# A planned instruction order, with transfers that hold the queue by their size and later assumed landings

## The chip, the cores and the metric

The kernel runs on one core of a Trainium2 chip. The metric is device time in microseconds; three runs of the kernel before gave 2084.32, 2087.18 and 2086.25 us, median 2086.25. One further execution was recorded by the hardware profiler.

## The reference, cut to what matters

128 graphs of 128 nodes with 256 features go through two layers. In layer 0 three rounds of a gated graph network run on `h`, and in layer 1 an attention over edges:

```python
h = relu(layernorm(x))
for i in range(3):                                   # layer 0
    m    = einsum('bnd,de->bne', h, weight[i])
    aggr = einsum('bst,bsd->btd', adj != 0, m)
    h    = gru_cell(aggr, h, w_ih, w_hh, b_ih, b_hh)
x = x + h
h  = relu(layernorm(x))                              # layer 1
Wh = h @ W ; s = Wh.sum(-1)
e  = where(adj == 0, -inf, leaky_relu(s[:, :, None] + s[:, None, :], 0.2))
x  = x + einsum('bpq,bqo->bpo', softmax(e), Wh)
```

## The kernel before, in words

The graphs are taken in 32 groups of four (`G = 4`). A group's node rows are 128 x 1024 float32 (512 KB) in a tile `rows`, its edges 256 KB in `at`; later `x` is read a second time into `x1` for the residual sum, and `x1` is written out (512 KB). Every round of a group is one "turn" on TensorE: products of node features with weights (L887 and L901) in seven-product blocks, which build up in the PSUM banks `x_rz, x_n, y_rz, y_n, q_rz, q_n`; ScalarE copies a bank out (L933, L937, L939) before TensorE may write it again. Edge sums are the 128x128 bf16 products of L807; the attention's products are L840 and L1326. The list `turns` interleaves the rounds: a group's round 0, the previous group's round 1 and the round 2 of the group before that follow one another.

Layer norms (`normed`, L686 to L702) run on VectorE (bn_stats, L686, four to a group), GpSimd (L695, L696) and ScalarE (L702). In the attention of a group VectorE reduces the scores to their maximum (L1243), negates a bounded form of it into `low` (L1245), ScalarE takes exponentials (L1250), copies them in halves into `pe` (L1422), a transfer transposes them (L1423, `peT`), and ScalarE unpacks them (L1426). Feature halves are transposed in the same way through `pl` and `plT` (L743, L753, L747). All transfers, transposes included, are issued by SyncE (SP), in one queue.

Nothing of the order is left to a scheduler at run time. `Plan.op` records each operation with its engine, its duration in ns, the tiles it reads and writes and a due time. `Plan.search` then tries many list schedules with random changes of rank (fixed seed), in windows, and keeps the one with the least idle TensorE, plus a tenth of `risk` (how far a TensorE operation has less than `SLACK` = 1500 ns of reserve); near the end, the modelled end counts too. The instructions are emitted in that order, and each engine runs its own in order. So a number in the plan changes no instruction, only places in five queues.

The lines that the change touches are those that say when a transfer's result may be used. An operation on SP holds the queue for its `ns`. Its users start no earlier than its end plus a lag (3600 ns where none is given) plus 28 ns. Landings are kept apart by a constant:

```python
FLIP, HANDOFF, COLD, BEHIND = 56, 120, 7200, 1200            # L57, in Plan
def wait(self, i, u):                                        # L141
    a, b = self.nodes[i], self.nodes[u][0]
    return 0 if a[0] == b == "PE" else a[7] + self.SIGNAL[b]
if e == "SP":                                                # L323, in go
    late = max(s.landed + self.BEHIND - done - n[7], 0)
    s.landed = done + n[7] + late
```

The loads of a group's `rows` and `at` are L1112 (L502 for the first four groups, `TIMED`), the second reading of `x` is L1131, the transposes L753 and L1423, the weight loads L502 and L571.

Of the kernel before, what the change touches and what calls it, by code (L numbers as in the profile page):

```python
# [16 lines left out]
P = 128  # L17
# [14 lines left out]
FIRST, LAST, COMMIT, AHEAD, SLACK, RISK = 20000, 120000, 32000, 40000, 1500, 0.1  # L32
TIMED = 4
KB = 3
GATES = 18150
BIG = 3.0e38

# [9 lines left out]
class Plan:  # L47
# [7 lines left out]
    LAG = {"PE": 163, "ACT": 0, "DVE": 0, "POOL": 0, "SP": 3600}  # L55
    OVER = {"PE": 0, "ACT": 50, "DVE": 40, "POOL": 0, "SP": 0}
    TRUE = {"PE": 0, "ACT": 103, "DVE": 84, "POOL": 42, "SP": 0}  # L57
    FLIP, HANDOFF, COLD, BEHIND = 56, 120, 7200, 1200
    SIGNAL = {"PE": 53, "ACT": 36, "DVE": 36, "POOL": 78, "SP": 28}

    def __init__(self, tags):
# [30 lines left out]
        return deps  # L92

    def op(self, eng, ns, fn, reads=(), writes=(), room=(), due=None, mark=None,
           turn=None, two=False, lag=None, thin=False):

        i, deps = len(self.nodes), set()  # L100
        self.group_of.append(self.group)
        for item in room:
            b, lo, hi = item if isinstance(item, tuple) else (item, 0, 1 << 30)
            if self.tags[b.tag][1] == "ring":
                self.rooms.append((i, b, lo, hi))
            elif b.prev is not None:
                deps.update(self.over(b, lo, hi))
        for is_write, group in ((False, reads), (True, writes)):
            for item in group:
                b, lo, hi = item if isinstance(item, tuple) else (item, 0, 1 << 30)  # L110
                for j, w, l, h in b.accesses:
                    if (w or is_write) and l < hi and lo < h:
                        deps.add(j)
                if is_write and b.prev is not None:
                    deps.update(self.over(b, lo, hi))
        for is_write, group in ((False, reads), (True, writes)):
            for item in group:
                b, lo, hi = item if isinstance(item, tuple) else (item, 0, 1 << 30)
                b.accesses.append((i, is_write, lo, hi))
        deps.discard(i)  # L120
        bufs = {id(x[0] if isinstance(x, tuple) else x): (x[0] if isinstance(x, tuple) else x)
                for x in list(reads) + list(writes) + list(room)
                if self.tags[(x[0] if isinstance(x, tuple) else x).tag][1] in ("free", "turn")}
        free = [b for b in bufs.values() if self.tags[b.tag][1] in ("free", "turn")]
        for b in free:
            b.users.append(i)
            b.left += 1
        self.nodes.append([eng, ns, fn, deps, free, self.due if due is None else due,
                           two or eng == "POOL", self.LAG[eng] if lag is None else lag, thin])
        if due is not None:  # L130
            self.chain.append(i)
        if mark is not None:
            self.marks[mark] = i
        if turn is not None:
            self.turns.append((i, turn))
# [2 lines left out]

        return self.nodes[i][1] * (2 if self.nodes[i][0] == "PE" and t < self.COLD else 1)

    def wait(self, i, u):  # L141

        a, b = self.nodes[i], self.nodes[u][0]
        return 0 if a[0] == b == "PE" else a[7] + self.SIGNAL[b]

    def run(self):
        nodes, self.queue = self.nodes, {}
# [99 lines left out]
    def go(self, s, until):  # L247

        nodes, users, bound, order_of = self.nodes, self.users, self.bound, self.others
        rank, slots, at, clock, ready = s.rank, s.slots, s.at, s.clock, s.ready  # L250
        inf = float("inf")
        while len(s.order) < len(nodes) and clock["PE"] < until:
            best = None
            nxt = order_of[s.chain] if s.chain < len(order_of) else None
            for e, pool in ready.items():
# [3 lines left out]
                c = clock[e]  # L259
                for i in pool:  # L260
                    n = nodes[i]
                    if i in bound and i != nxt:
                        continue
                    t = max(c + (self.FLIP if s.thin and e == "PE" and not n[8] else 0), at[i])
                    if n[4]:
                        new = {}
                        for b in n[4]:
                            if id(b) not in s.slot:
                                new[b.tag] = new.get(b.tag, -1) + 1
                                t = max(t, sorted(slots[b.tag])[new[b.tag]])  # L270
                                if b.tag in self.queue and self.queue[b.tag][s.turn[b.tag]] is not b:
                                    t = inf
# [6 lines left out]
                asked, i = min(((r, i) for t, r, i in starts if t <= first), key=lambda x: (rank[x[1]], x[1]))  # L279
# [5 lines left out]
            t, _, e, i = best  # L285
# [3 lines left out]
            n = nodes[i]  # L289
            asked, cause, kind = s.other[i] if e == "PE" else at[i], s.due_to[i], "dep"  # L290
            done = t + self.ns(i, t)
            for b in n[4]:
                if id(b) not in s.slot:
                    if b.tag in self.queue:
                        s.turn[b.tag] += 1
                    k = min(range(len(slots[b.tag])), key=lambda k: slots[b.tag][k])
# [24 lines left out]
            s.end = max(s.end, done)  # L321
            late = 0
            if e == "SP":  # L323
                late = max(s.landed + self.BEHIND - done - n[7], 0)
                s.landed = done + n[7] + late
            for u in users[i]:
                s.missing[u] -= 1
# [41 lines left out]
def kernel(  # L369
# [21 lines left out]
    nc = tc.nc  # L391
# [58 lines left out]
    def ap(b):  # L450
        return phys[(b.tag,) + b.slot]
# [12 lines left out]
    op, buf = plan.op, plan.buf  # L464
# [32 lines left out]
        plan.group = SETS - 1  # L497
        return buf(tag)

    def load(dst, get, src, kb, behind=(), lag=3300):  # L500

        op("SP", kb * KB, lambda: nc.sync.dma_start(get(dst), src), behind, [dst], lag=lag)  # L502

    def plain(b):
        t = ap(b)
# [47 lines left out]
    def weights():  # L553
# [5 lines left out]
            return plain(b).rearrange("p (k e) -> p k e", k=KD)  # L559

        def load_msg(layer, behind=()):
            load(w_msg[layer], square, weight[layer].rearrange("(k p) e -> p k e", p=P), 256,
                 behind)


        plan.due = -2 * 10 ** 9
# [2 lines left out]
        for a in range(2):  # L569
            part = slice(3 * a, 3 * a + 3)  # L570
            op("SP", 384 * KB, lambda part=part: nc.sync.dma_start(  # L571
                nat(w_ih_nat)[:, part], w_ih.rearrange("(c p) e -> p c e", p=P)[:, part]),
               [], [(w_ih_nat, a, a + 1)], lag=3300 + 700 * a)
        plan.due = 10 ** 9
        load(w_hh_nat, nat, w_hh.rearrange("(c p) e -> p c e", p=P), 768, lag=5000)
        plan.due = -10 ** 8
        load_msg(1)
        plan.due = 10 ** 9
# [172 lines left out]
    def transpose(pl, plT, k, n):  # L751

        op("SP", 1283, lambda: nc.sync.dma_start_transpose(  # L753
            ap(plT)[:, k, 0:n].rearrange("p c (m q) -> p (c m) q", q=P),
            ap(pl)[:, k, 0:n].rearrange("p c m -> p (c m)")), [(pl, k, k + 1)], [(plT, k, k + 1)],
           lag=2200)

    def parts_of(rows):

# [342 lines left out]
    def group(g):  # L1102
        graphs = slice(g * G, (g + 1) * G)
        plan.phase = phase(g, 0)
        plan.due = (plan.phase - 1) * SLOT
        rows0, at, a, hT = buf("rows"), buf("at"), buf("a"), buf("hT")
        for t, src, kb in ((rows0, x[graphs].rearrange("b n d -> n b d"), 512),
                           (at, adj[graphs].rearrange("b n m -> n b m"), 256)):
            if g < TIMED:
                load(t, ap, src, kb, lag=4800 if t is at else 3300)  # L1110
            else:
                op("SP", 480, lambda t=t, src=src: nc.sync.dma_start(ap(t), src), [], [t])  # L1112
        op("DVE", 420, lambda: nc.vector.tensor_scalar(ap(a), ap(at), 0.0, None,
                                                       op0=OP.not_equal), [at], [a], two=True)
        plan.due = (phase(g, L - 1) + 2) * SLOT
        normed(rows0, rows0)
        for layer in range(L):
            plan.phase = phase(g, layer)
            if layer == 0:
                if g < EARLY:  # L1120
                    rows_to_T(rows0, hT)
                else:
                    turned_halves(rows0, True, hT)
                parts = parts_of(rows0) if g >= WHOLE else (rows0, buf("r1"))
            elif layer < L - 1:
                parts = turned_parts(hT)
            else:
                rows, x1, h1 = buf("rows"), buf("x1"), buf("h1")
                turned_halves(hT, False, rows)
                parts = parts_of(rows)  # L1130
                op("SP", 480, lambda: nc.sync.dma_start(  # L1131
                    ap(x1), x[graphs].rearrange("b n d -> n b d")), [], [x1])
            hs, aT, gs = buf("hs"), buf("aT"), buf("gs")
            node_sums(hT, hs, "POOL", 1272, 730)
            edge_sums(parts, a, aT)
            node_sums(aT, gs, "DVE", 690, 426)
            plan.cursor = plan.phase * SLOT
            if layer < L - 1:
                gru(layer, hT, hs, aT, gs)
        plan.due = min(phase(g, L - 1) + 3, len(turns) + 0.5) * SLOT  # L1140
        gru_rows(L - 1, hT, hs, aT, gs, rows, x1)
        if g < NG - 1:
            attention(g, lambda: edges_of(g, a), x1, h1, 0, G)
        else:
            scores = edges_of(g, a)
            for lo, hi in ((G // 2, G), (0, G // 2)):
                attention(g, lambda: scores, x1, h1, lo, hi)
# [271 lines left out]
    def turned_halves_of(halves, src, dst):  # L1419

        pe, peT = buf("pe"), buf("peT")
        op("ACT", 1045, lambda: nc.scalar.copy(ap(pe), halves()), [src], [pe])  # L1422
        op("SP", 1283, lambda: nc.sync.dma_start_transpose(  # L1423
            ap(peT).rearrange("p two g q -> p (two g) q"),
            ap(pe).rearrange("p two g m -> p (two g m)")), [pe], [peT], lag=2200)
        op("ACT", 1347, lambda: nc.scalar.copy(halves_of_blocks(dst), ap(peT)), [peT], [dst])  # L1426

    weights()
# [34 lines left out]
```

## Time and profile before

| what | us |
|---|---|
| median of three runs | 2086.25 |
| profiled execution, its time | 2087.59 |
| profiled execution, span from first to last instruction | 2085.5 |
| TensorE matmul busy | 2069.2 |
| VectorE / ScalarE / GpSimd busy | 1688.3 / 1619.1 / 910.0 |
| issue to landing, median: `rows` 512 KB | 5.1 |
| the same: second reading `x` 512 KB | 4.3 |
| the same: `at` 256 KB | 2.8 |
| the same: transposes plT / peT | 3.3 / 3.2 |

Busy time of TensorE includes modelled ends of pipelined matmuls, so a short gap can be partly covered by them; where it matters, gaps are read from start to start. In lists of waits the columns are: engine and line that waited, what released it, microseconds in total, times, longest. In a timeline or chain they are start, length, then the work; a bracket holds the idle time before it and its releaser. The stretch table gives, for each stretch, its length, then busy time and number of instructions of TensorE matmuls, TensorE weight loads, VectorE, ScalarE and GpSimd, the granted TensorE clock, the DMA share and GB/s.

### The profile page before, as it was taken

To read this page: it belongs to the slowest core of one execution; us is meant where nothing else is said; L and a number is where in the kernel's file an instruction comes from. 1 tells how busy PE (TensorE), PEld (TensorE's weight loads), DVE (VectorE), ACT (ScalarE), POOL (GpSimd) and SP (SyncE) were. 2 spreads that over 40 slices of the span, in tenths; PEclk is the share of its full clock that TensorE was granted. 3 is DMA by queue.
4 is the path that set the end of the run, shared out by engine and by line. 5 is a ranking of instruction groups with operands and counts; after the bars stand their busy time and mean duration, and the time that the engine had idled before them with its cause. 6 is when DMAs were issued, how large, how long until landed. Compare 5 with 4: busy or idle time off the path is not lost.

```text
span 2085.5 us, 31660 instructions
## 1 busy us (share of the span) xinstructions
PE 2069.2 (99%) x10926; PEld 1660.3 (80%) x10926; DVE 1688.3 (81%) x3912; ACT 1619.1 (78%) x3007; POOL 910.0 (44%) x885
## 2 busy tenths in 40 slices
PE   9999999999999999999999999999999999999998
PEld 7887887778877778877788877788777888788875
DVE  6777887888878888887888887888888877788677
ACT  6677887788877788877888777878777886878775
POOL 4644544435434435444354434454443544445330
PEclk9999999999999999999999999999999999999999
DMA  5322233332333323233222333232333223323321
GB/s 147 66 64 43 56 69 72 73 69 43 69 74 71 76 47 71 61 79 73 65 49 66 82 66 76 49 64 66 76 76 61 46 67 77 61 44 67 64 66 36
DMA packets 369376, 138.12 MB, mean 66 GB/s; under 512 B 300608, under 2 KB 368960, under 8 KB 369216
## 3 DMA queue, kind: packets, MB, share of 16 engines
q1 hardware_dynamic: 369216, 136.10, 29.6%
q8 instruction: 86, 1.41, 0.3%
q14 instruction: 74, 0.61, 0.1%
HBM read 45.36 MB, written 16.78 MB: 30 GB/s over the span
## 4 chain that ended last, share of the span: by engine, by line
PE 94%; DMA 2%; ACT 1%; DVE 1%; POOL 1%; SPq 0%; issue 0%; ACTq 0%; DVEq 0%; POOLq 0%
PE y_rz L887 15%; PE q_rz L887 10%; PE x_rz L887 10%; PE y_n L887 7%; PE misc L807 6%; PE y_n L901 6%; PE y_rz L901 6%; PE q_n L887 5%; PE x_n L887 5%; PE misc L1326 4%; PE x_n L901 4%; PE q_n L901 4%; PE x_rz L901 4%; PE q_rz L901 4%; PE misc L840 3%; DMA rows<-in_x_dram 2%
## 5 line engine op out<-in xcount | busy, mean ns | idle before, releaser
L856 POOL TENSOR_TENSOR hs<-hT 128x512 f32<-128x512 f32 x96 | 123.0, 1282 | 466.4 <-PE y_n L901 244.9
L764 POOL TENSOR_TENSOR r<-rows 128x512 f32<-128x512 f32 x126 | 137.7, 1111 | 173.0 <-ACT rows L702 91.0
L887 PE MATMUL y_rz<-hs,s_hh 128*128 128x256 f32 x768 | 197.7, 380 | 3.6 <-ACT t_rz L933 3.6
L887 PE MATMUL y_rz<-gs,s_x 128*128 128x256 f32 x768 | 197.2, 379 | 0.0
L943 DVE TENSOR_TENSOR t_rz<-t_rz,q_rz 128x512 f32<-128x512 f32 x192 | 131.4, 684 | 77.2 <-ACT t_rz L933 55.6
L933 ACT COPY t_rz<-y_rz 128x512 f32<-128x512 f32 x192 | 112.0, 583 | 99.9 <-PE y_rz L901 60.7
L887 PEld LDWEIGHTS y_rz<-hs,s_hh 128*128 128x128 f32 x768 | 145.3, 190 | 25.4 <-POOL rs L695 2.8
L860 POOL TENSOR_TENSOR hs<-hT,hs 128x256 f32<-128x256 f32 x96 | 77.6, 809 | 198.2 <-PE q_n L901 160.1
L887 PEld LDWEIGHTS y_rz<-gs,s_x 128*128 128x128 f32 x768 | 145.9, 190 | 19.6
L767 POOL TENSOR_TENSOR p<-r 128x512 bf16<-128x512 f32 x126 | 155.1, 1248 | 2.7
L943 DVE TENSOR_TENSOR t_n<-t_n,q_n 128x512 f32<-128x512 f32 x192 | 131.1, 683 | 29.5 <-PE q_n L901 17.1
L1081 POOL TENSOR_TENSOR x<-x,u 128x512 f32<-128x512 f32 x60 | 78.8, 1315 | 139.6 <-ACT u L1061 139.6
L887 PE MATMUL x_rz<-aT,s_x 128*128 128x256 f32 x512 | 131.5, 379 | 0.0
L887 PE MATMUL x_rz<-hT,s_hh 128*128 128x256 f32 x512 | 131.4, 379 | 0.0
L1017 ACT ACTIVATE u<-u,bias_i 128x512 f32<-128x512 f32 x128 | 91.1, 723 | 36.3 <-DVE u L1008 36.3
L887 PE MATMUL y_n<-hs,s_hh 128*128 128x256 f32 x384 | 114.4, 380 | 0.0
L887 PE MATMUL y_n<-gs,s_x 128*128 128x256 f32 x384 | 114.2, 379 | 0.0
L856 DVE TENSOR_TENSOR gs<-aT 128x512 f32<-128x512 f32 x96 | 91.0, 948 | 27.9 <-ACT aT L813 27.8
L887 PEld LDWEIGHTS x_rz<-hT,s_hh 128*128 128x128 f32 x512 | 97.2, 190 | 19.1
L1338 DVE SCALAR_TENSOR_TENSOR x<-misc,rden,x 128x128 f32<-128x128 f32 x312 | 89.6, 344 | 27.9 <-ACT rz L1043 15.0
L887 PEld LDWEIGHTS x_rz<-aT,s_x 128*128 128x128 f32 x512 | 97.1, 190 | 13.0
L789 POOL TENSOR_TENSOR pl<-d,pl 128x512 bf16<-128x512 f32 x64 | 83.5, 1313 | 50.9 <-ACT pl L787 50.7
(296 smaller groups left out, 6390.4 us busy)
## 6 DMA issues: line engine op xcount, KB each, us to landing
rows<-in_x_dram SPq DMA_DIRECT2D x32, 512.0 KB, 5.1
x<-in_x_dram SPq DMA_DIRECT2D x32, 512.0 KB, 4.3
out_dram<-x SPq DMA_DIRECT2D x31, 512.0 KB, 2.9
at<-in_adj_dram SPq DMA_DIRECT2D x32, 256.0 KB, 2.8
plT<-pl SPq DMA_TRANSPOSE x190, 3.3
peT<-pe SPq DMA_TRANSPOSE x60, 3.2
e<-in_L_gnn_weight_dram SPq DMA_DIRECT2D x3, 256.0 KB, 4.2
rz<-in_L_gnn_w_ih_dram SPq DMA_DIRECT2D x2, 384.0 KB, 4.2
```

Source lines behind the costliest of these rows:

```text
L764: op("POOL", 1042, lambda part=part: nc.gpsimd.tensor_tensor(ap(r1)[:, part], ap(rows)[:, part], top(rows)[:, part], OP.subtract), [(rows, ...
L767: op("POOL", 1042, lambda part=part: nc.gpsimd.tensor_tensor(ap(p3)[:, part], ap(r1)[:, part], top(r1)[:, part], OP.subtract), [(r1, n, n ...
L789: op("POOL", 1158, lambda k=k, r=r: nc.gpsimd.tensor_tensor(part(pl, k, 2), ap(r), part(pl, k, 1), OP.subtract), [r], [(pl, k, k + 1)])
L807: nc.tensor.matmul(flat(pair[k])[:, b * N:(b + 1) * N], part(i, b, k), ap(a)[:, b, :], start=(b == 0 and i == 0), stop=(i == 2), skip_grou ...
L856: op(eng, cost, lambda: sub(ap(w)[:, 0:2, :], blocks()[:, 1::2, :], blocks()[:, 0:2, :], OP.subtract), [t], [(w, 0, 2)], two=True)
L887: nc.tensor.matmul(ap(bank)[:, half, :], ap(w)[:, i - 1, gate, :], source(i, t, sums), start=(first and c == 0 and m == 0), stop=False, sk ...
L901: op("PE", 645, lambda c=c, w=w, t=t, sums=sums: nc.tensor.matmul(flat(bank)[:, c * P:(c + 3) * P], source(i, t, sums)[:, m * N:(m + 1) * ...
L933: op("ACT", 590, lambda: nc.scalar.copy(ap(t), ap(y)), [y], [t], mark=mark)
L943: op("DVE", 690, lambda: nc.vector.tensor_tensor(ap(t), ap(t), ap(q), OP.add), [q], [t])
L1017: op("ACT", 723, lambda j=j, cols=cols: nc.scalar.activation(ap(u)[:, cols], ap(u)[:, cols], AF.Tanh, bias=ap(W["bias_i"])[:, 2 * KD + j:2 ...
L1326: nc.tensor.matmul(ap(b)[:, h, m * P:(m + 1) * P], source(i, uT, sums)[:, m * N:(m + 1) * N], ap(W["w1"])[:, c], start=(first and m == 0), ...
L1338: op("DVE", 340, lambda i=i, m=m: nc.vector.scalar_tensor_tensor(ap(x1)[:, i, j * P:(j + 1) * P], ap(b)[:, h, m * P:(m + 1) * P], ap(rden) ...
```

## The change

Operations get two more numbers: `takes`, how far behind the landing before it a landing is kept (1200 by default, for loads 2.85 ns for each KB: 1459 for 512 KB, 730 for 256 KB), and `spare`, a time that is added for all users of the operation. `wait` (now `twait` plus `spare`) uses it in ranks and in the schedule. The loads of the first four groups, of the weights and of the transposes get other lags. No operation is added or taken away; the two programs have the same instructions on each engine, in another order.

```diff
+SERVICE = 2.85
+X_SPARE, AT_SPARE, T_SPARE = 3400, 2500, 400
...
     def op(self, eng, ns, fn, reads=(), writes=(), room=(), due=None, mark=None,
-           turn=None, two=False, lag=None, thin=False):
+           turn=None, two=False, lag=None, thin=False, takes=1200, spare=0):
...
-    def wait(self, i, u):
+    def twait(self, i, u):
 
         a, b = self.nodes[i], self.nodes[u][0]
         return 0 if a[0] == b == "PE" else a[7] + self.SIGNAL[b]
+
+    def wait(self, i, u):
+
+        return self.twait(i, u) + self.nodes[i][10]
...
-                late = max(s.landed + self.BEHIND - done - n[7], 0)
+                late = max(s.landed + n[9] - done - n[7], 0)
...
-    def load(dst, get, src, kb, behind=(), lag=3300):
+    def load(dst, get, src, kb, behind=(), lag=2300):
 
-        op("SP", kb * KB, lambda: nc.sync.dma_start(get(dst), src), behind, [dst], lag=lag)
+        op("SP", kb * KB, lambda: nc.sync.dma_start(get(dst), src), behind, [dst],
+           lag=lag, takes=kb * SERVICE)
...
-            load(w_msg[layer], square, weight[layer].rearrange("(k p) e -> p k e", p=P), 256,
-                 behind)
+            load(w_msg[layer], square, weight[layer].rearrange("(k p) e -> p k e", p=P),
+                 360 if layer == 1 else 256, behind, 2300 if layer else 2800)
...
-               [], [(w_ih_nat, a, a + 1)], lag=3300 + 700 * a)
+               [], [(w_ih_nat, a, a + 1)], lag=2700, takes=1100 + 1350 * a)
-        load(w_hh_nat, nat, w_hh.rearrange("(c p) e -> p c e", p=P), 768, lag=5000)
+        load(w_hh_nat, nat, w_hh.rearrange("(c p) e -> p c e", p=P), 768, lag=4200)
...
             ap(pl)[:, k, 0:n].rearrange("p c m -> p (c m)")), [(pl, k, k + 1)], [(plT, k, k + 1)],
-           lag=2200)
+           lag=1950, spare=T_SPARE)
...
             if g < TIMED:
-                load(t, ap, src, kb, lag=4800 if t is at else 3300)
+                load(t, ap, src, kb, lag=2300 if t is at else 3500)
             else:
-                op("SP", 480, lambda t=t, src=src: nc.sync.dma_start(ap(t), src), [], [t])
+                op("SP", 480, lambda t=t, src=src: nc.sync.dma_start(ap(t), src), [], [t],
+                   lag=2400 if t is at else 3600, takes=kb * SERVICE, spare=AT_SPARE if t is at else X_SPARE)
...
                 op("SP", 480, lambda: nc.sync.dma_start(
-                    ap(x1), x[graphs].rearrange("b n d -> n b d")), [], [x1])
+                    ap(x1), x[graphs].rearrange("b n d -> n b d")), [], [x1],
+                   takes=512 * SERVICE, spare=X_SPARE)
...
             ap(peT).rearrange("p two g q -> p (two g) q"),
-            ap(pe).rearrange("p two g m -> p (two g m)")), [pe], [peT], lag=2200)
+            ap(pe).rearrange("p two g m -> p (two g m)")), [pe], [peT], lag=1850, spare=T_SPARE)
```

More of the change, by code (lines that the diff above doesn't have):

```diff
@@ L57 @@
     TRUE = {"PE": 0, "ACT": 103, "DVE": 84, "POOL": 42, "SP": 0}
-    FLIP, HANDOFF, COLD, BEHIND = 56, 120, 7200, 1200
+    FLIP, HANDOFF, COLD = 56, 120, 7200
     SIGNAL = {"PE": 53, "ACT": 36, "DVE": 36, "POOL": 78, "SP": 28}
@@ L128, in op @@
         self.nodes.append([eng, ns, fn, deps, free, self.due if due is None else due,
-                           two or eng == "POOL", self.LAG[eng] if lag is None else lag, thin])
+                           two or eng == "POOL", self.LAG[eng] if lag is None else lag, thin, takes, spare])
         if due is not None:
```

## The prediction

> **What bounds the kernel now.** I read the page's busy shares first, then the stretch table, which says where TensorE is not busy, then the list of who TensorE waited for, and last the chain of waits and the timeline around one such wait.
>
> ```profile
> PE 2069.2 (99%) x10926; PEld 1660.3 (80%) x10926; DVE 1688.3 (81%) x3912; ACT 1619.1 (78%) x3007; POOL 910.0 (44%) x885
> ...
> PEclk9999999999999999999999999999999999999999
> ```
>
> ```profile
> 0.00:25.00 25.00, 20.91 (x100) 14.04 (x101) 16.34 (x47) 11.72 (x24) 9.48 (x16) 1.00 0.73 221
> 25.00:2055.00 2030.00, 2025.87 (x10722) 1629.68 (x10721) 1651.28 (x3798) 1593.52 (x2940) 898.32 (x866) 1.00 0.30 65
> 2055.00:2085.50 30.50, 22.46 (x108) 16.55 (x106) 20.63 (x68) 13.88 (x43) 2.16 (x4) 0.97 0.16 52
> ```
>
> TensorE is the bound everywhere, at full clock. It is idle 4.1 us in the first 25 us, 4.1 us in the 2,030 us between, and 8.0 us in the last 30.5 us: 16.3 us in all, 0.8% of the span. The change takes no arithmetic away, so this, with what the modelled matmul ends hide, is all it can win. The middle has one cause:
>
> ```profile
> PE y_rz L887 <- ACT t_rz L933: 3.6, 6, 0.9
> PE misc L1326 <- DVE h L1308: 0.4, 1, 0.4
> ```
>
> The chain of waits over 520 to 545 us shows what is behind one of these six (start, length, work):
>
> ```profile
> 530.42 5.15 DMA rows<-in_x_dram
> 535.57 0.02 issue
> 535.60 1.41 DVE st L686 x4
> 537.00 0.28 DVE mv L691 x4
> 537.28 0.83 DVE low L1245
> 538.12 0.02 issue
> 538.14 1.28 ACT e L1250 x4
> 539.42 0.36 ACT rz L1011
> 539.78 0.36 ACT rz L993
> 540.14 0.48 ACT t_rz L933
> 540.62 0.14 issue
> 540.75 1.97 PE y_rz L887 x8
> ```
>
> The node rows of the next group are not needed by TensorE for a long time. But VectorE runs in the written order, its bn_stats (L686) stands ahead of the attention bound `low` (L1245), and so the landing holds up `low`, the exponentials, the copy that frees bank y_rz, and TensorE. The timeline gives the landing that is too late and what it costs:
>
> ```profile
> 535.60 1.41 DVE L686 BATCH_NORM_STATS2 st<-rows 128x6 f32<-128x256 f32 x4 [2.06 <-DMA rows<-in_x_dram]
> 540.75 1.10 PE L887 MATMUL y_rz<-hs,s_hh 128*128 128x256 f32 x4 [0.54 <-ACT t_rz L933]
> ```
>
> **Step 1: the rows' landing.** The planner of before lets a user of a `rows` load start 480 + 3600 + 28 ns = 4.1 us after its issue. Measured, issue to landing has a median of 5.1 us, and bn_stats starts 4.0 to 6.5 us after the issue in most groups (7.1 once). VectorE waits for rows 37.1 us in 25 waits, 1.5 us each, 3.6 at most. Most of that is absorbed: in the group at 912 us the wait is 1.70 us, the copy t_rz ends at 922.54, TensorE wants the bank at 923.02, so 0.5 us is left. Waits with a longer tail go through.
>
> A rule speaks against any gain. The Trainium skill, page "DMA: Bandwidth & Descriptors", section "Anatomy of one DMA", prices a transfer at 2.0 us plus its bytes over 436 GB/s (fitted on GpSimd's path, not on SP's queue as here). For 512 KB that is an estimate of 3.2 us; with the `x` load issued 0.62 us before it, 2.0 + 2 x 1.2 - 0.62 = 3.8 us. Either is inside the 4.1 us, so by the rule the stalls could not exist and the step would be worth 0. The rows say 5.1 and up to 6.5; I take the rows.
>
> What it costs: in each case the last x_n matmuls show when the next should have started (pairs are 0.43 us apart). At 540.75 it should have been 540.05: 0.70 us. The others, 349.27, 605.23, 987.21, 1178.05 and 1369.85 us, lost 0.60, 0.78, 0.65, 0.14 and 1.10: 3.97 us in six. The first four matmuls after each take 1.10 instead of 1.03 us, 6 x 0.07 = 0.4. Sum 4.4 us. (Five of these are in the row of 3.6 us; the sixth there, 0.59 at 143.64, comes from a late transpose and is counted below.)
>
> After, the allowance is 480 + 3600 + 28 + 3400 = 7.5 us, and a landing is kept 1.46 us from the one before. The order lists of the two programs show what became of it. The `rows` load stands at the same place in SP's queue in 30 of 32 groups; bn_stats stands 5.4 VectorE instructions later on average in groups 4 to 27, nearly always behind `low`. At 0.43 us each (1688.3/3912) and 81% busy that is 5.4 x 0.53 = 2.9 us, against waits of 1.5 us. In the typical group bn_stats now follows L997, which at 912 us comes after 921.6, 9 us after the issue. The stall is gone: -4.4 us (bounds -5.0, -3.0). What is late next: nothing near. bn_stats (1.41 us) goes in where VectorE waited for the copy t_rz, and ScalarE's normalisation (L702) of these rows moves by one to three instructions only.
>
> **Step 2: what moves ahead.** With `low` early the planner puts the exponentials (L1250) earlier and also the 1.06 us copy `pe` (L1422) ahead of the t_rz copy, in about 20 groups. Measured pieces from the group at 912: `low` can end by 917.1 (GpSimd's L1081 runs until 917.0, and `low` was seen to run beside GpSimd work in 0.8 us) and ScalarE takes L1250 behind the t_rz copy of 917.18, at 917.8; then 1.2 + 0.4 + 0.4 + 0.4 + 0.4 + 1.06 + 0.57, end at 922.2 against 923.02. Slack 0.8 us instead of 0.5: cost 0. Uncovered, it costs 0.3 to 0.6 us in each of 20 groups. Kept for the slower rival.
>
> **Step 3: transposes, edge loads, second x load.** The allowance of plT goes from 2200 to 1950 + 400, of peT to 1850 + 400, 0.15 and 0.05 us later; issue to landing is 3.3 and 3.2 us, allowance before 3.5. `at` gets 480 + 2400 + 2500 instead of 4.1 us and lands in 2.8. SP's queue changes places by two or three at most in steady state. Behind a waiting SP instruction there are only transfers, and SP's own waits do not reach TensorE in the middle. Bounds -0.3 to +1.0; I take 0, the row with no such wait.
>
> **Step 4: the start.** Idle TensorE in the first 25 us: 1.25 before anything, 0.61 for w_ih, 0.61 for the second message weight, 0.24 for ScalarE's uT copy, 1.24 for VectorE's hT copy. The first seven loads stand in the same order, so the DMA waits stay. The first product now goes to x_rz, not to the bank that ScalarE is still emptying: -0.4 us. In exchange more weight products and their VectorE copies run before the first rows: from durations of the start's timeline I get waits of 0.4, 0.2, 0.2 to 1.0, 0 to 0.7 and about 1.0 us in a row where there was one of 1.4. Bounds -0.4 to +2.0, taken +0.5. In the first turns the wait of 0.59 at 143.64 has no counterpart I can place: bounds -0.7 to +1.0, taken -0.2.
>
> **Step 5: the end.** The last 30 us are ordered anew. By hand, with the durations of that timeline: the bound of the last but one group comes 0.3 us earlier and its exponentials with it; the normalisation of the last group's first half 0.2 later, of the second about 0.6 earlier. Bounds -1.2 to +1.2, taken -0.4.
>
> **Sum.** The profiled execution took 2087.59 us (span 2085.5). 2087.59 - 4.4 + 0 + 0 + 0.5 - 0.2 - 0.4 = 2083.1; plus 0.2 for small new misfits = 2083.3 us. The runs shown have a median of 2086.25, 1.3 below the profiled one; their spread of 2.9 us is what some landings stalling and some not would give, so I take part of that difference as stalls already missing in the median, not as a lower floor. Against the median the forecast is -3.0 us, -0.14%. Less than 0.2% (4.2 us: about 2082.1 to 2090.4) cannot be told from no change here.
>
> **Rivals.**
> - *More than the rows' stalls goes* (start and end also tighten): -4.4 - 1 at the end - 1 at the start and the first turns gives 2080.8 us. For: 12 of the 16.3 idle us are there. Against: they follow from the order of dependent steps at both ends, which landing times hardly touch.
> - *The change doesn't do what it says*: the allowance only moves the waits, and the random search gives the gain back in new stalls of its own. 2087.6 - 4.4 + 3.4 = 2086.6. For: each order has a few misfits (0.59, 0.4 in this one). Against: the misfits of before outside the rows sum to about 1.5 us.
> - *Slower*: step 2's copy L1422 holds the t_rz copy. It decides when L1250 starts later than about 918.6 in the group at 912, 6.0 us after the rows' issue; a start 0.4 us beyond that costs 0.4 + 0.07 us in 20 groups, 9.4 us: 2087.6 - 4.4 + 0.5 + 9.4 = 2093.1. For: `low` measured 0.83 us where it is a 0.15 us operation. Against: the planner left 0.8 us by measured pieces.
>
> **How the numbers follow.** Forecast 0.52 (2081.5 to 2085.5; a quarter of it below 2082.1), more 0.25, moved 0.12, slower 0.11 (nearly all beyond 2090.4). Faster 0.13 + 0.25 = 0.38; slower 0.10; the rest, 0.52, within 0.2%. The range 2080.0 to 2088.0 leaves out about 0.1 on each side.
>
> **What would show it.** Right: the wait of VectorE for rows falls from 37.1 to under 10 us; the y_rz wait on t_rz in the middle falls from 3.6 to under 1 us; TensorE idle between 25 and 2055 us under 2 us; matmul busy time the same within 2 us; idle at both ends as before within 1 us each. Wrong: a repeated y_rz wait behind L1422, a new wait of more than 0.3 us in many groups, a first 25 us with more than 6 us idle, or rows landing later than before.

## The result and the profile after

| | us |
|---|---|
| before, median of 17 runs beside it (2084.32 to 2087.44) | 2086.64 |
| after, median of 17 runs (2081.07 to 2084.73) | 2081.78 |
| ratio after/before, 95% interval | 0.998 (0.9972 to 0.9987) |
| forecast | 2083.3, range 2080.0 to 2088.0 |
| profiled execution of after: time, span | 2084.73, 2082.9 |

The kernel became faster by 0.2% (0.13 to 0.28%). The profiled execution of after is the longest of its 17, 2.95 us above their median, so it was profiled a second time (first experiment; 2083.17 us, span 2081.4). Where the two differ, both are shown.

The stretch table of after (first profile; length, then busy us and instructions of TensorE, its weight loads, VectorE, ScalarE, GpSimd, then the granted clock, the DMA share and GB/s):

```profile
0.00:25.00 25.00, 20.98 (x90) 14.09 (x91) 14.21 (x47) 10.95 (x23) 7.86 (x15) 0.93 0.66 200
25.00:2055.00 2030.00, 2028.86 (x10745) 1633.90 (x10744) 1658.28 (x3804) 1602.42 (x2948) 911.00 (x867) 1.00 0.30 65
2055.00:2082.93 27.93, 19.59 (x94) 13.82 (x92) 17.67 (x61) 12.20 (x37) 1.78 (x4) 0.96 0.17 57
```

Idle TensorE is 4.0 us in the first 25 us (4.1 before), 1.1 in the middle (4.1 before), and 8.3 at the end (8.0 before). Matmul busy time is 2069.4 us against 2069.2. VectorE's wait for rows fell from 37.1 us in 25 waits to 0.7 in one (0.9 in the second profile). So the gain is in the middle, as foreseen. TensorE's waits in the middle (engine and line, releaser, us in total, times, longest):

```profile
PE misc L1335 <- ACT misc L1353: 1.0, 2, 0.5
```

Only one other, of 0.2 us, is listed. The wait for y_rz is gone. The two waits at L1335 are new: the chain of waits in front of the first goes back to a transpose of features that landed 3.7 us after its issue, for which ScalarE's copy L750 waited 2.05 us, with the bank copy L1353 queued behind. The timeline of the group at 913 us (after, second profile) shows what took the place of the stall (start, length, engine and line, work):

```profile
913.50 1.02 DVE L1254 TENSOR_SCALAR low<-top 128x4 f32<-128x4 f32 x1
...
915.03 1.39 DVE L693 BATCH_NORM_STATS2 st<-rows 128x6 f32<-128x256 f32 x4
```

```profile
915.15 1.28 ACT L1259 ACTIVATE e<-e,low 128x128 f32<-128x128 f32 x4
...
917.04 1.05 ACT L1431 COPY pe<-e 128x1024 uint16<-128x1024 uint16 x1
917.97 0.60 ACT L940 COPY t_rz<-y_rz 128x512 f32<-128x512 f32 x1
```

```profile
919.50 1.03 PE L894 MATMUL y_rz<-hs,s_hh 128*128 128x256 f32 x4
```

`low` runs before bn_stats, neither has a bracket with a wait for rows, the copy `pe` now stands ahead of the t_rz copy, and that copy still ends at 918.57, 0.9 us before TensorE takes the bank. Over all steady groups, measured issue by issue: in before `low` starts 6.8 us after the issue of the rows (median) and bn_stats 5.1; in after `low` at 4.1 and bn_stats at 8.2. The median distance from the end of the t_rz copy to TensorE's next y_rz product is 0.49 us in before (six of 21 groups at 0.14, which is a stall) and 0.94 in after (smallest 0.26).

### The profile page after: what moved, and what is told of

It reads as the page before. It is cut to its first block, busy times and chain, and to the rows that moved or that the text cites. A ratio compares the mean times of both kernels' runs of the same rounds, so it can differ in the third digit from the quotient of the medians.

```text
span 2082.9 us, 31644 instructions
## 1 busy us (share of the span) xinstructions
PE 2069.4 (99%) x10926; PEld 1661.8 (80%) x10926; DVE 1690.2 (81%) x3912; ACT 1625.6 (78%) x3007; POOL 920.6 (44%) x885
## 4 chain that ended last, share of the span: by engine, by line
PE 97%; ACT 1%; DMA 1%; DVE 1%; issue 0%; POOL 0%; SPq 0%; ACTq 0%; DVEq 0%; POOLq 0%
PE y_rz L894 16%; PE x_rz L894 11%; PE q_rz L894 10%; PE y_n L894 8%; PE misc L814 6%; PE y_n L908 6%; PE y_rz L908 6%; PE x_n L894 5%; PE q_n L894 5%; PE misc L1335 4%; PE q_n L908 4%; PE x_n L908 4%; PE q_rz L908 4%; PE x_rz L908 4%; PE misc L847 2%; PE misc L1295 1%
## 5 line engine op out<-in xcount | busy, mean ns | idle before, releaser
L771 POOL TENSOR_TENSOR r<-rows 128x512 f32<-128x512 f32 x126 | 158.9, 1272 | 179.8 <-ACT rows L754 48.3
L894 PE MATMUL y_rz<-hs,s_hh 128*128 128x256 f32 x768 | 197.2, 379 | 0.0
L894 PE MATMUL y_rz<-gs,s_x 128*128 128x256 f32 x768 | 197.1, 379 | 0.0
L867 POOL TENSOR_TENSOR hs<-hT,hs 128x256 f32<-128x256 f32 x96 | 73.0, 761 | 202.2 <-PE q_n L908 159.6
L894 PEld LDWEIGHTS y_rz<-gs,s_x 128*128 128x128 f32 x768 | 145.9, 190 | 19.8
L894 PEld LDWEIGHTS y_rz<-hs,s_hh 128*128 128x128 f32 x768 | 144.0, 190 | 18.6
L774 POOL TENSOR_TENSOR p<-r 128x512 bf16<-128x512 f32 x126 | 148.1, 1186 | 4.8
L894 PE MATMUL x_rz<-aT,s_x 128*128 128x256 f32 x512 | 131.4, 379 | 0.0
L894 PE MATMUL x_rz<-hT,s_hh 128*128 128x256 f32 x512 | 131.4, 379 | 0.0
L894 PE MATMUL y_n<-hs,s_hh 128*128 128x256 f32 x384 | 114.3, 379 | 0.0
L894 PE MATMUL y_n<-gs,s_x 128*128 128x256 f32 x384 | 114.2, 379 | 0.0
L894 PEld LDWEIGHTS x_rz<-hT,s_hh 128*128 128x128 f32 x512 | 97.1, 190 | 19.1
L1027 DVE TENSOR_TENSOR d<-hT,u 128x512 f32<-128x512 f32 x128 | 101.9, 800 | 8.5 <-ACT u L1024 7.4
L863 DVE TENSOR_TENSOR gs<-aT 128x512 f32<-128x512 f32 x96 | 85.5, 891 | 28.2 <-ACT aT L820 27.3
L894 PEld LDWEIGHTS x_rz<-aT,s_x 128*128 128x128 f32 x512 | 97.1, 190 | 13.1
```

Of the source, the lines that this page charges most:

```text
L771: op("POOL", 1042, lambda part=part: nc.gpsimd.tensor_tensor(ap(r1)[:, part], ap(rows)[:, part], top(rows)[:, part], OP.subtract), [(rows, ...
L774: op("POOL", 1042, lambda part=part: nc.gpsimd.tensor_tensor(ap(p3)[:, part], ap(r1)[:, part], top(r1)[:, part], OP.subtract), [(r1, n, n ...
L863: op(eng, cost, lambda: sub(ap(w)[:, 0:2, :], blocks()[:, 1::2, :], blocks()[:, 0:2, :], OP.subtract), [t], [(w, 0, 2)], two=True)
L894: nc.tensor.matmul(ap(bank)[:, half, :], ap(w)[:, i - 1, gate, :], source(i, t, sums), start=(first and c == 0 and m == 0), stop=False, sk ...
L1027: op("DVE", 690, lambda j=j, d=d, cols=cols: nc.vector.tensor_tensor(ap(d), ap(hT)[:, j, :], ap(u)[:, cols], OP.subtract), [(hT, lo, hi), ...
```

## The experiments

All were timed in five rounds beside the kernel before; a ratio below is to before on the same chip, with its 95% interval. "Middle" is the time from the start of the first product of L901 to the end of the last one, taken as 0.32 us after its start: 1908.05 us in before. A kernel with added lines has other line numbers: before's L887 and L901 are L894 and L908 in after, L891 and L905 in the second experiment, and L898 and L912 where bn_stats is put back ahead.

### The changed kernel again

No edit.

> The changed kernel once more, unaltered, to see an ordinary execution of it: its profiled execution of 2084.73 us is the longest of 17 and 2.95 above their median of 2081.78. Theory (the extra lies in the start): the median is 2081.8 +- 0.5, and in the new profile the first 25 us show about 2 us less idle than that one's and TensorE's first wait for w_ih is below 1 us where it was 2.07. Rival (the extra lies in the middle or the tail): the first 25 us are as long as in that profile and the difference stands in other waits.

Measured: 2081.70 us, ratio 0.9979 (0.9972 to 0.9987); profiled execution 2083.17, 1.4 us shorter than the first. Both profiles wait about 2 us for the second half of w_ih. The timelines of TensorE's start, first profile and then second:

```profile
8.52 0.77 PE L530 MATMUL misc<-ident,rz 128*128 128x128 f32 x3 [2.07 <-DMA rz<-in_L_gnn_w_ih_dram]
...
10.57 1.77 PE L632 MATMUL x_rz<-x,uT 128*128 128x256 f32 x4
```

```profile
8.05 0.52 PE L530 MATMUL misc<-ident,rz 128*128 128x128 f32 x3 [1.93 <-DMA rz<-in_L_gnn_w_ih_dram]
...
9.57 1.03 PE L632 MATMUL x_rz<-x,uT 128*128 128x256 f32 x4
```

After 2.07 us the same four products take 1.77 us, after 1.93 us they take 1.03. The stretch from 10 to 12 us has a granted clock of 0.50 in the first and 1.00 in the second. By the time the first product of a group round starts (the first q_rz product) the first profile is 1.75 us behind, and it stays there (1.54 at the end). So the theory holds as to place, not as to cause: the wait itself did not get shorter than 1 us.

Against before, this profile divides so: up to the first product of L901 147.78 us against 148.93 (-1.15), middle 1904.18 (-3.87), from there to the end 29.43 against 28.52 (+0.91).

### Before, with bn_stats behind `low` and nothing else

```diff
 # after planning, in 23 groups by the trace; other engines keep their order
-[bn_stats(rows) x4, bn_aggr x4, low]
+[low, bn_stats(rows) x4, bn_aggr x4]
```

> Before's own plan; after planning, only the bn_stats and bn_aggr on the rows of the next group (24 groups) are moved from ahead of the masking step `low` to behind it in VectorE's order. TensorE, ScalarE, GpSimd and the DMA queue keep before's order. Theory (the six waits on y_rz come from bn_stats that waits for its rows ahead of `low`): the wait for y_rz in the middle falls from 3.6 us to below 0.5, TensorE's idle time between 25 and 2055 us from 4.1 to about 0.5, and the time to 2086.6 - 4.0 = 2082.6 (2081.8 to 2083.4). Rival (the gain of the change is a new plan of start and tail, and the six waits would come back elsewhere): 2086.2 to 2087.0, unchanged.

Measured: 2082.91 us, 0.9986 (0.9979 to 0.9992), so -3.2 us (-1.7 to -4.4). The profile of this kernel: the y_rz waits of TensorE in the middle, and the timeline of the group that stalled 0.70 us at 540.75 in before:

```profile
PE y_rz L891 <- ACT t_rz L937: 0.5, 1, 0.5
```

```profile
533.65 0.53 DVE L1250 TENSOR_SCALAR low<-top 128x4 f32<-128x4 f32 x1
535.51 1.40 DVE L688 BATCH_NORM_STATS2 st<-rows 128x6 f32<-128x256 f32 x4 [1.32 <-DMA rows<-in_x_dram]
```

```profile
540.09 1.03 PE L891 MATMUL y_rz<-hs,s_hh 128*128 128x256 f32 x4
```

bn_stats still waits for the rows here, 1.32 us in this group, but nothing that TensorE needs stands behind it. Middle 1903.63 us: -4.42. What is left (0.5) is the wait at 143.64 of before, which has another cause. This shows the mechanism with one thing changed: the place of bn_stats in one engine's order.

### Before, with the allowance for the rows alone

```diff
-op("SP", 480, lambda t=t, src=src: nc.sync.dma_start(ap(t), src), [], [t])
+op("SP", 480, lambda t=t, src=src: nc.sync.dma_start(ap(t), src), [], [t],
+   spare=0 if t is at else 3400)
```

> Before with one of the change's numbers alone: the planner adds 3.4 us to the landing of the rows of a steady group for all that use them. First loads, edge loads, second x loads and transposes are planned as before. Theory (this one number carries the gain): the wait for y_rz in the middle below 0.5 us, 2082.6 (2081.5 to 2084). Rival (the gain needs the other numbers as well, or the rest of the change gives it): 2085 to 2087.

Measured: 2083.09 us, 0.9986 (0.998 to 0.9993). No y_rz wait in the middle; the one wait left there is 0.9 us for the copy aT; smallest distance behind a t_rz copy 0.29 us. The one number does what the step said. By the medians 1.4 us of the change's gain are missing, but the two intervals overlap.

### After, with bn_stats put back ahead of `low`

```diff
 # after's plan, after planning
-[low, ..., bn_stats(rows) x4, bn_aggr x4]
+[bn_stats(rows) x4, bn_aggr x4, low, ...]
```

> The changed kernel's plan; after planning, only the bn_stats and bn_aggr on the rows are put back ahead of the masking step `low` in VectorE's order. Everything else of the change stays. Theory: the waits on y_rz return, in as many groups or more than before (six of 24 at 0.1 to 1.1 us each, since the rows land as late after their issue as they did), so 2081.8 + 3 to 6 = 2085 to 2088. Rival (start, tail and transposes carry the gain): 2081.5 to 2082.5, unchanged.

Measured: 2101.52 us, 1.0075 (1.0063 to 1.0088): 20 us slower than after, where 3 to 6 were expected. The direction is right and the size is a miss. Waits of TensorE in the middle:

```profile
PE y_n L898 <- ACT t_n L950: 8.6, 8, 2.0
PE y_rz L898 <- ACT t_rz L944: 3.8, 9, 0.9
PE y_rz L898 <- POOL hs L867: 1.3, 5, 0.3
```

These are more than the stalls of before, although the rows land as they did (bn_stats 5.1 us after the issue, `low` 6.7). So after's plan spends the early `low`: it puts ScalarE work that needs `low` ahead of bank copies. Read from start to start, the waits for y_n sum to about 10 us and those for y_rz to about 7; a wait of 2.00 us among them is followed by half clock, about 1.7 us more (last section).

### The same, with the `pe` copy moved behind the bank copies: two attempts

> The changed kernel's plan with bn_stats and bn_aggr of the rows put back ahead of `low`, as in the run that took 2101.5, and in addition the 1.05 us copy `pe` of the attention weights moved behind the two bank copies t_rz and t_n that it was planned ahead of. In that run TensorE waited 13.7 us for the banks y_rz and y_n in 22 places; in the group at 922 us bn_stats waits for its rows, `low` comes 6.6 us after the issue of the rows instead of 4.1, and the t_rz copy ends 3.98 us after the start of `low` where it ended 2.91 us after it in before, the difference being the `pe` copy. Theory (late bn_stats costs 4 to 5 us, and the remaining 10 come from the `pe` copy that stands in the slack): about 2085.5 to 2088, the two waits together at 3 to 5 us. Rival (the extra comes from other places of the plan, such as ScalarE's or GpSimd's new order): 2098 to 2102, as before the move.

Measured: 2102.12 us, 1.0074 (1.0061 to 1.0086). In this kernel the copy had stayed where it was in all 19 steady groups, so it repeats the run before it (0.6 us apart) and tells nothing about `pe`.

```diff
 # after's plan with bn_stats ahead of low; ScalarE, 20 groups
-[pe<-e (and its transpose on SP), t_rz<-y_rz, t_n<-y_n]
+[t_rz<-y_rz, t_n<-y_n, pe<-e (and its transpose on SP)]
```

> The experiment that the run at 2102.1 us failed to make: there the `pe` copy stayed ahead of the bank copies in all 19 steady groups, because its transpose already stood ahead of them in the order; only one copy near the start moved. Here the copy and its transpose are moved together, behind both bank copies, in 20 groups; bn_stats and bn_aggr of the rows stay ahead of `low`. Theory (late bn_stats alone costs 4 to 5 us over the changed kernel, the other 15 come from the `pe` copy that was moved ahead into the slack): 2085.5 to 2088, waits on y_rz and y_n in the middle together 3 to 5 us. Rival (the 15 us lie in other places of the plan): 2097 to 2102, waits above 10 us.

Measured: 2096.42 us, 1.0055 (1.0042 to 1.0068). 5 us come back, not 15. The waits show which part (this profile is the longest of the five runs, 5.4 us above their median):

```profile
PE y_n L898 <- ACT t_n L951: 8.9, 7, 2.0
PE y_rz L898 <- ACT t_rz L945: 1.4, 2, 0.8
```

The `pe` copy was the cause of most of the y_rz waits (from 14 times to 2). The y_n waits stayed; the chain of waits in the group at 604 us of this kernel (start, length, work) shows theirs:

```profile
595.98 6.38 DMA rows<-in_x_dram
...
602.39 1.41 DVE st L695 x4
603.79 0.28 DVE mv L700 x3
604.07 0.43 DVE low L1260
...
604.52 1.28 ACT e L1265 x4
605.80 0.36 ACT t_n L949
606.16 0.27 ACT t_n L951
...
606.47 1.13 PE y_n L898 x4
```

In some groups after's plan has the exponentials ahead of the t_n copy that frees bank y_n. With `low` on time (after, group at 595 us) they end at 597.7 and cost nothing; with `low` held by a landing TensorE waits. Seven or eight groups are of this kind. Neither theory had named it.

### Parts of the change

First loads only (edit of after):

```diff
 # transposes plT, peT
-lag=1950, spare=T_SPARE
-lag=1850, spare=T_SPARE
+lag=2200
 # steady rows, at, second x: takes, spare and lag dropped
```

> The changed kernel with its new costs for the first loads only (weights, and rows and edges of the first four groups); steady loads and transposes are costed as before the change. Theory (the start is worth about 1.1 us by the trace of the changed kernel, and the waits on y_rz stay): 2084.5 to 2086.5, y_rz waits in the middle of 2 to 5 us. Rival (the first loads carry the gain): 2081 to 2083, no y_rz waits.

Steady loads and transposes only (edit of after):

```diff
-def load(dst, get, src, kb, behind=(), lag=2300):    # with takes=kb * SERVICE
+def load(dst, get, src, kb, behind=(), lag=3300):    # without
 # w_msg, w_ih, w_hh and the timed rows and at: lags of before
```

> The changed kernel with the new costs for steady loads and transposes only; the first loads are costed as before. Theory: no y_rz waits in the middle, the start as in before (first products of layer 0 some 1.1 us later than in the changed kernel), so 2082 to 2084. Rival (spares without the new start do nothing): 2085 to 2087.

First loads and the rows' allowance (edit of "first loads only"):

```diff
-op("SP", 480, lambda t=t, src=src: nc.sync.dma_start(ap(t), src), [], [t])
+op("SP", 480, lambda t=t, src=src: nc.sync.dma_start(ap(t), src), [], [t],
+   spare=0 if t is at else X_SPARE)
```

> The changed kernel with two parts only: new costs of the first loads, and 3.4 us more for the rows of the steady groups. Edge loads, second x loads and transposes are costed as before. Theory (the rows carry about 4 us, the first loads 1, and the rest of the change nothing but two new waits of 0.4 us for ScalarE): 2080.5 to 2082.5. Rival (the other allowances matter): 2083 or more, or waits behind edge loads or transposes in the middle above 2 us.

| kernel | median us | ratio (95%) | y_rz waits on t_rz in the middle, us (times) |
|---|---|---|---|
| first loads only | 2083.92 | 0.9987 (0.9981 to 0.9994) | 1.3 (3) |
| steady loads and transposes only | 2082.44 | 0.9981 (0.9972 to 0.9989) | none |
| first loads and rows' allowance | 2082.78 | 0.9982 (0.9974 to 0.9989) | 0.9 (1), at an L908 product; other waits 2.3 |

"Late only" has nearly all of the gain, as expected. "First only" is 0.6 us below its expected range: it keeps the old allowance for the rows, yet is 2.7 us faster than before. In its profile the part up to the first product of L901 is 1.95 us shorter, and the middle 1.49 (1906.56), with three y_rz waits where before had six. "First and rows" is 0.3 above its range. The parts do not add: each is a new draw of the random search, and this is what the last pair tests.

### Other seeds of the planner's search

```diff
-Random(1)
+Random(2)        # or Random(3)
```

> The changed kernel with another seed of the planner's random search; costs and allowances unchanged. Theory (the allowance for the rows, not a lucky plan, removes the waits): no y_rz wait behind t_rz and the rows in the middle, 2080.5 to 2083.5. Rival (luck of the plan): y_rz waits of 2 us or more again, 2084 or more.

> The kernel of before with another seed of the planner's random search. Theory: bn_stats stands ahead of `low` again and waits for its rows, y_rz waits in the middle of 1 to 5 us, 2084.5 to 2088. Rival (before was an unlucky plan): no such waits and 2081 to 2083.5.

> The kernel of before with a third seed of the planner's random search, to see the spread of plans made with the old allowance. Theory: y_rz waits in the middle of 1 to 5 us, 2084.5 to 2088. Rival (before was an unlucky plan): no such waits and 2081 to 2083.5.

| plan | median us | ratio (95%) | y_rz waits on t_rz in the middle, us (times) |
|---|---|---|---|
| after, seed 2 | 2082.81 | 0.9983 (0.9975 to 0.9991) | 0.5 (1), at an L908 product |
| before, seed 2 | 2083.60 | 0.9988 (0.9981 to 0.9994) | 0.8 (2) |
| before, seed 3 | 2082.61 | 0.9983 (0.9975 to 0.999) | none |

Here the rival wins, with seed 3 in full and with seed 2 nearly (0.1 us above the rival's range, 0.8 us of waits): the plan of before was an unlucky one. In before's costs with seed 3, VectorE still waits for the rows, and TensorE does not. VectorE's wait for rows and TensorE's whole list in the middle, seed 3:

```profile
DVE st L686 <- DMA rows<-in_x_dram: 25.8, 21, 2.1
```

```profile
PE y_n L887 <- ACT t_n L933: 0.7, 1, 0.7
PE y_rz L887 <- POOL hs L856: 0.3, 1, 0.3
```

The reason can be read group by group. From the rows' issue the chain is about 5.1 us to bn_stats, 1.6 to `low`, 3.3 to the end of the t_rz copy: 10.0 us. In most groups of all these plans TensorE wants the bank 10.5 us after the issue, so 0.5 is left. Some groups are planned with 9.3 to 9.8, which the old landing time allows (4.1 + 1.6 + 3.3 = 9.0). In before there are five such groups, and four of them stall by 0.14 to 1.10; the other two stalls are landings of 6.5 us against 10.3. Seed 2 has three such groups, of which one stalls by more than 0.1 us (0.64), and a stall of 0.44 at 10.2. Seed 3 has two, and in both the last part happened to take 2.7 to 2.8 us; it has one stall in such a chain (0.42, behind GpSimd).

## Why the prediction was right, and where its sum was off

**Direction and size.** Forecast 2083.3, measured 2081.78 in the first set of runs and 2081.70 in the second; -0.14% forecast against before's median of then, -0.23% measured. Each sign that was named for being right came: the waits of VectorE for rows and of TensorE for y_rz went, the middle has 1.1 us of idle TensorE, and both ends are as before within 1 us. The time lies below 2082.1, where the forecast put 0.38 of the chance, and nearer to "more goes" than to the forecast, but not for that rival's reason, which wanted a shorter end. (Its 2080.8 is summed wrongly: 2087.6 - 4.4 - 1 - 1 is 2081.2.) What made the difference is not a stall but the base of the sum. The steps sum to -4.3 us; with the second profile it is 2087.59 to 2083.17, -4.42, and median against median (second set) 2086.15 to 2081.70, -4.45. The first profile would give -2.86 and the first set of medians -4.86, so the close agreement is partly chance. The forecast took 2087.59 - 4.3 as the median to come, and argued that part of the 1.3 us between before's profiled execution and its median were stalls that the median already lacked. The runs do not bear that out: in after, which has no such stalls, the second profiled execution lies 1.47 above the median and the runs still spread over 3.7 us. Taken from the median, 2086.25 - 4.3 = 2082.0. In the 13 executions profiled after the forecast the profiled one lies between 2.0 below and 5.4 above the median, so the offset of one profile says nothing of the next plan's.

**Step 1, -4.4 (bounds -5.0 to -3.0): right.** The edit that moves bn_stats alone takes 4.42 us from the middle of its profile, and 3.2 (1.7 to 4.4) from the median. The rule that priced the landing at 3.2 to 3.8 us, and so the step at 0, is refuted by this case's runs: where bn_stats follows the landing closely, it starts 5.0 to 5.1 us after the issue in the median group of every plan.

**Step 2, 0: right, and narrower than it looked.** The slack forecast was 0.8 us; it is 0.94 in the median group. The last but one experiment prices what stands behind it: with `low` held until 6.7 us after the issue, the moved `pe` copy and exponentials cost 20 us (the slower rival had 9.4 for the `pe` copy alone, from 6.0 us on; the copy's share measured 5.1). The working named the copy `pe` and missed the exponentials ahead of the t_n copy.

**Step 3, 0 (bounds -0.3 to +1.0): about +0.5.** Two waits of 0.4 to 0.5 us behind late transposes came in (0.57 and 0.71 from start to start in the first profile), and one of 0.4 at L1326 went. The sum held 0.2 for new misfits. With step 1 this makes the middle -3.87, against -4.2 forecast.

**Step 4, +0.3 in all (+0.5 and -0.2): -1.15.** In the second profile the first 25 us have 3.97 us of idle TensorE (4.09 before), not more, and the wait of 0.59 at 143.64, taken at -0.2, went wholly. The working had five waits in a row at the first rows; the list has one of 0.6 us (L833). It had the transfer waits as before; in their place the wait for the second half of w_ih grew from 0.61 to 1.93 us, while that for the second message weight (0.61) went. This growth need not be the order's doing: issued at about 1.75 us in all 14 profiles, that half landed anywhere from 6.79 us (before) to 8.39 (after, first profile), and at 8.17 in the profile of before with bn_stats behind, whose first loads are those of before. So -1.15 sets an early landing against a late one, and single profiles of the start carry more than 1 us of such difference. The first product to x_rz shows no wait, as it said.

**Step 5, -0.4 (bounds -1.2 to +1.2): +0.9.** TensorE's waits listed in the last stretch sum to 4.6 us against 4.1. The wait at L847 (0.7) is not new, it is L840 of before. New are 0.5 for `rden` (q_rz, L1413), 0.5 for uT (y_rz, L1388) and 0.3 at L1202, while the wait for uT at L1295 (L1286 of before) fell from 0.7 to 0.2. Why the stretch grew by 0.4 more than its listed waits is not shown. Steps 4 and 5 are off by -1.45 and +1.3, which nearly cancels; that the sum of -4.3 met -4.4 owes something to this.

**What was not asked.** The forecast took it that the change is worth what the stalls cost. As a change of these two plans that holds. As a property of the allowance it holds only in part: the old allowance gave 2086.1, 2083.9, 2083.6 and 2082.6 us in four plans (with before's or after's first loads), the new one for the rows 2081.7, 2082.4, 2082.8, 2082.8 and 2083.1 in five. The means differ by 1.5 us, with a spread of 3.5 us within the first set. Whether that difference would stand over many seeds is open. None of the experiments is clearly faster than after itself.

## What to carry to other kernels

When a planner's cost is corrected, look in the new order for what the correction allowed to move ahead: here each engine's order after the change relies on `low` being on time, and a landing that held it would cost four times what was won. Before crediting a corrected cost with a gain, replan both versions with another seed or two: one plan in four carried most of the stalls. And take a forecast from the median by the difference that the profile gives, not from the profiled execution's own time.

## What the runs showed of the hardware

Waits of TensorE of up to 1.99 us left the granted clock at 1.00: 1.79 us in the last kernel with bn_stats ahead (606 us), 1.93 at the start of after's second profile, 1.99 in the first attempt on `pe` (1380 us). Four waits of 2.00 to 2.25 us were followed by a granted clock of 0.50: 2.07 at the start of after's first profile, 2.00 in each of the other two kernels with bn_stats ahead, 2.25 in before with seed 2 (2059 us). The timeline of one of them (after with bn_stats ahead and `pe` behind, at 1375 us):

```profile
1375.33 0.70 PE L898 MATMUL y_n<-hs,s_hh 128*128 128x256 f32 x2 [2.00 <-ACT t_n L951]
...
1377.84 1.91 PE L898 MATMUL y_rz<-hs,s_hh 128*128 128x256 f32 x4
...
1380.58 0.59 PE L898 MATMUL y_n<-hs,s_hh 128*128 128x256 f32 x2
```

The slow products begin about 1.1 us after the restart; from 1376.5 to 1379.8 us the granted clock is 0.50. From the restart to the last line shown are 5.25 us, where the same products after the wait of 1.79 us took 3.56, so the slow clock adds 1.7 us to the wait. The Trainium skill, page "TensorE: Matmul & The Clock Gate", section "Why this matters for your kernels", asks only that gaps stay under about 3 us; here gaps of 2.00 to 2.25 us were enough, so a wait of 2 us can cost about 3.7. The length of one wait is not the whole condition: at 2076 us of the same kernel half clock set in behind waits of 0.32 and 0.67 us alone. What decides there is open.
